# Expert rows added to the residual by accumulating DMA transfers, in a four-layer gated cross-attention kernel

## The chip, the cores and the metric

The kernel runs on one core of a Trainium2 chip. The metric is the time of one execution on the device, in microseconds (us). The engines are PE (matrix multiplication), DVE (vector), ACT (scalar, activation functions), POOL (the general engine, which also issues DMA transfers of its own) and SP (here only an issuer of DMA transfers). Each engine works through its own queue in order and waits at semaphores for the others.

## The reference, cut to what matters

The state `x` is 16 sequences of 128 tokens with 256 features. Four layers follow each other, each a cross attention against a context of 128 positions per sequence (layer 3: 8 heads of 64, layers 0 to 2: 16 heads of 16) and a feed-forward part, both added through a gate:

```python
x = x + jnp.tanh(g_xattn[0]) * _L0_xattn_ref(ctx_1024, _layernorm(x, axis=-1), ctx_1024, ...)
x = x + jnp.tanh(g_ffn[0]) * _L0_ffn_ref(_layernorm(x, axis=-1), ...)
x = x + jnp.tanh(g_xattn[1]) * _L1_xattn_ref(_layernorm(x, axis=-1), ctx_1024, ctx_1024, ...)
...
x = x + jnp.tanh(g_ffn[3]) * _L3_ffn_ref(_layernorm(x, axis=-1), ...)
return x
```

The feed-forward parts of layers 0, 2 and 3 are mixtures of 8 experts; each token goes to its best two, and their outputs are added with the router's weights. In layer 0:

```python
gate = jax.nn.softmax(flat_x @ w_gate.T, axis=-1)
topk_scores, topk_idx = jax.lax.top_k(gate, TOP_K)
cw = (jax.nn.one_hot(topk_idx, N_EXPERTS, dtype=flat_x.dtype) * topk_scores[..., None]).sum(axis=1)
h = jax.nn.gelu(jnp.einsum('td,edh->teh', flat_x, W1) + b1, approximate=False)
y = jnp.einsum('teh,ehd->ted', h, W2) + b2
out = jnp.einsum('ted,te->td', y, cw)
```

Layer 1 has a dense layer with eight low-rank additions instead. In layer 1's attention the softmax runs over the queries and not over the keys.

## The kernel before, in words

The residual lies in SBUF as 16 tiles `xs[b]` of 128 tokens x 256 features, one per sequence. The sequences go in 4 blocks of 4 (NBLK = 4, BPB = 4).

**Attention.** `attend()` (L1282) writes the order of work on PE, ACT, DVE by hand. It walks over the 16 sequences of a layer (of two layers where they follow each other without an expert stage between, layers 1 and 2). A step of a sequence computes scores (ps_s, L1191), exponentials on ACT (e, L1206), sums on DVE (L1215, in layer 1 with v scaled by their reciprocals, L1218 and L1220), the product with v (ps_o, L1246), its copy to SBUF (oT, in layer 1 a DVE copy, L1254), the output projection (ps_y, L1267) and the addition to the residual (L358), after which `ready(b)` takes the mean and variance of the sequence's rows (L237, L238).

Between these, at set points, `tick()` lets *jobs* go on: Python generators which issue a piece of other work and say with `yield n` after how many ticks they want to be called again. The number is capped: `job[1] = min(next(job[0]), most[late])`, with `most` = (5, 1) in layer 0, (99, 1) in layers 1 and 2, (2, 1) in layer 3; `late` is set when the last sequence's step has begun its tail, so that from then on each job goes on at every tick. The jobs are the next block's `prepare` (layer norm, transposes, queries) and the block just finished's `behind` (the router). In the tail, a filler, the first slots of the expert stage, is put in after the jobs of each tick.

**Router.** `front()` (L428) of a mixture takes a block of 4 sequences: layer norm (ACT xn, L298), `yield 4` (L315), transposes on PE (ps_ln, L321), router matmuls (L405), the two largest (DVE, up to `both`, L456), `yield 6` (L457), rank matmuls (ps_rank, L461), then 8 indirect DMAs from POOL (L516) that scatter the block's rows into `xg` in DRAM, sorted by expert. A `plan` (L572 to L660, DVE) says which slot has which expert; plans are made early after the blocks, and the last after block 3.

**Slots.** `slots()` (L671) works on 39 slots of 128 rows of one expert: SP loads the rows (xr, L733) and the expert's weights (1 MB each, L1352), `turn(s)` transposes the rows on PE (ps_xr, L766) and copies them on DVE (xT, L768), `hidden` makes the hidden activations (L1399 in layer 0, L1624 in layer 3), `finish` multiplies with the second weight (ps_e, L803), weighs the rows on DVE (y, L809 and L811) and scatters them from POOL into `yd` in DRAM (L815). There `yd` has two rows per token, one per expert. The first slots (9 in layer 0, 17 in layer 3) run as filler in the attention's tail while later blocks still are being routed; the rest follow. Before slot 0's hidden matmuls stand `turn(0)` and `turn(1)` (L831, L832; `turn` is L760).

**Fetch.** The next layer's attention (layers 1 and 3) first has to add these rows. `fetch()` (L541) does it in `prepare` of each block: SP loads the two rows of each token (yr, 256 KB per sequence, L547), four ticks later two DVE additions per sequence (L552), `ready(b)`, and a tick between sequences. After layer 3, `last()` (L525) does the same on DVE and POOL and stores the output.

**POOL** zeroes `xg` at the start by direct DMAs (L2149), issues the scatters, clears the v tiles of an attention (L1105) and adds up sums or reciprocals of each sequence (`watch.see`, L1060, tile sum_range) for a check of the range; the tiles which it reads have two buffers. If the values leave the range, a second, slower path is run; the fast one (`run["fast"]`) is the one measured.

Of the kernel before, what the change touches and what calls it, by code (L numbers as in the profile page):

```python
# [12 lines left out]
ALU = mybir.AluOpType  # L13
# [7 lines left out]
B = 16  # L21
S = 128
D = 256
KC = D // P
NBLK = 4
BPB = B // NBLK
# [64 lines left out]
def kernel(ctx: ExitStack, tc: tile.TileContext, a: dict, out: bass.AP):  # L91
    nc = tc.nc
# [11 lines left out]
    xs = []  # L104
# [96 lines left out]

    def finish(job):

        while True:
            try:
                next(job)
            except StopIteration as end:
                return end.value  # L210
# [35 lines left out]
    def ready(b):  # L246

        blk, i = divmod(b, BPB)
        if run["fast"]:
            if i == 0:  # L250
                seen[blk] = new_mv()
            mean_var(seen[blk], i, xs[b])
# [52 lines left out]
    def block(blk):  # L305
        return range(blk * BPB, (blk + 1) * BPB)

    def ln_block(blk, see=None, own_set=False):


        mv, rstd = yield from ln_residual(blk, own_set=own_set)
        if see is not None:
            see(rstd)
        xns = yield from normalized([xs[b] for b in block(blk)], mv, rstd)
        yield 4  # L315
        xt = xtpool.tile([P, KC, TB], F32, tag="xnT", name="xnT")
        for pair in range(BPB // 2):
            ps = ps_x.tile([P, KC, 2 * S], F32, tag="x", name="ps_ln")
            for j in range(2):
                for k in range(KC):  # L320
                    nc.tensor.transpose(  # L321
                        ps[:, k, j * S:(j + 1) * S],
                        xns[:, pair * 2 + j, k * P:(k + 1) * P], ident,
                    )
            nc.scalar.copy(xt[:, :, pair * 2 * S:(pair + 1) * 2 * S], ps)
            yield 1 if pair == 0 else 3
        return xns, xt
# [86 lines left out]
    class Moe:  # L414
# [13 lines left out]
        def front(self, blk, plan=None):  # L428
# [25 lines left out]
            first_max(hot[:, 1], key2)  # L454
            both = small("both")
            nc.vector.tensor_tensor(both, hot[:, 0], hot[:, 1], ALU.add)  # L456
            yield 6  # L457


            ps = ps_x.tile([P, 2, BPB, NE], F32, tag="x", name="ps_rank")  # L460
# [79 lines left out]

        def fetch(self, pool, blk):  # L541

            rows2 = yd[:, :].rearrange("(j t) d -> t j d", j=2)
            ys = []
            for b in block(blk):
                y = pool.tile([P, 2, D], F32, tag="yr", name="yr", bufs=BPB)
                nc.sync.dma_start(out=y, in_=rows2[b * S:(b + 1) * S])  # L547
                ys.append(y)
            yield 4
            for i, b in enumerate(block(blk)):  # L550
                for j in range(2):
                    nc.vector.tensor_tensor(xs[b], xs[b], ys[i][:, j], ALU.add)  # L552
                ready(b)
                yield 1
# [116 lines left out]
        def slots(self, n, plans, lanes, get, fetch1, fetch2, hidden, nf, far, depth):  # L671
# [27 lines left out]
            def lane(s):  # L699
                return lanes[plan_of(s)[2]]  # L700
# [59 lines left out]
            def turn(s):  # L760
                if s >= n:
                    return
                xr = xrs[s]
                ps = ps_x.tile([P, KC, S], F32, tag="x", name="ps_xr")
                for k in range(KC):
                    nc.tensor.transpose(ps[:, k, :], xr[:, k * P:(k + 1) * P], ident)  # L766
                xT = get("xT", [P, KC, S])
                nc.vector.tensor_copy(xT, ps)  # L768
                xTs[s] = xT
# [59 lines left out]
                load(s)  # L829
            yield 1  # L830
            turn(0)  # L831
            turn(1)  # L832
            weigh(0)
            hidden_of = []
            for s in range(n):
                while not planned(s + far + 1):
                    yield 1
                first(s + near)
                hT = yield from hidden(get, lane(s), xTs.pop(s), lambda *ps: when(s, *ps))
                turn(s + 2)  # L840
                hidden_of.append((s, hT))
                if len(hidden_of) > depth:
                    finish(*hidden_of.pop(0))
                weigh(s + 1)
                load(s + far)
                second(s + near2)
                yield 1
# [230 lines left out]
    class Fast16:  # L1078
# [155 lines left out]
        def values(self, b, tick):  # L1234
            pool, v = self.pool, self.vs[b % 3]
            es = self.es.pop(b)
            oT = pool.tile([P, KC, S], F32, tag="oT", name="oT")


            po = ps_x.tile([P, 2, KC, S], F32, tag="x", name="ps_o")  # L1240
            for i in range(1 if self.layer == 1 else 2):
                for c in range(KC):
                    for e in range(2):
                        for j in range(4):
                            w = ones2[:, e].rearrange("p e d -> p (e d)")
                            nc.tensor.matmul(  # L1246
                                po[32 * j:32 * (j + 1), i, c, :],
                                lhsT=w if i else v[:, c * HPC + 2 * j + e, :],
                                rhs=es[j][:, 2 * c + e, :], start=(e == 0), stop=(e == 1),
                            )  # L1250
                if i == 0:
                    tick()
            if self.layer == 1:
                nc.vector.tensor_copy(oT, po[:, 0])  # L1254
            else:
                rs = pool.tile([P, KC, S], F32, tag="rs", name="rs")
                nc.vector.reciprocal(rs, po[:, 1])  # L1257
                self.watch.see(rs.rearrange("p c s -> p (c s)"))
                nc.vector.tensor_tensor(oT, po[:, 0], rs, ALU.mult)
            self.os[b] = oT  # L1260
            tick()
# [20 lines left out]
    def attend(parts, most=(99, 1), filler=None, open_end=False):  # L1282

        jobs = []  # L1290
        late = False
        filling = []

        def tick():
            for job in list(jobs) + filling:
                job[1] -= 1
                if job[1] <= 0:
                    try:
                        job[1] = min(next(job[0]), most[late])
                    except StopIteration:  # L1300
                        (jobs if job in jobs else filling).remove(job)

        def ahead(att, before, blk):
            made = att.prepare(blk, before(blk) if before is not None else None)
            made = [[job, 0] for job in made]
            jobs.extend(made)
            return made

        steps = [(att, b) for att, _, _ in parts for b in range(B)]
        blocks = [(att, before, behind, blk) for att, before, behind in parts  # L1310
                  for blk in range(NBLK)]
        with tc.manual_schedule(engines=IN_ORDER):
            ln_exp()
            prepared = ahead(*blocks[0][:2], 0)
            for n in range(len(steps) + 2):
                if n == len(steps) - 1 and open_end:
                    next(filler)
                if n == len(steps):
                    late = True
                    if filler is not None:  # L1320
                        filling.append([filler, 0])
                if n < len(steps):
                    if n % BPB == 0:

                        while any(job in jobs for job in prepared):
                            tick()
                        if n // BPB + 1 < len(blocks):
                            att, before, _, blk = blocks[n // BPB + 1]
                            prepared = ahead(att, before, blk)
                    att, b = steps[n]  # L1330
                    att.scores(b, tick)
                if 1 <= n <= len(steps):
                    att, b = steps[n - 1]
                    att.values(b, tick)
                if n >= 2:
                    att, b = steps[n - 2]
                    att.output(b, tick)
                    if b % BPB == BPB - 1:
                        _, _, behind, blk = blocks[(n - 2) // BPB]
                        jobs.append([behind(blk), 0])  # L1340
            while jobs or (filling and not open_end):
                tick()
# [722 lines left out]
    def layers(fast):  # L2065
# [16 lines left out]
        def routed(moe, turns, begin=None):  # L2082


            plans = []

            def make(blk):
                early = blk < NBLK - 1
                kind = str(len(plans)) if early else ""
                plans.append((yield from moe.plan(turns[blk], early, kind)))  # L2090
                if early and begin is not None:
                    begin(plans[-1])

            def behind(blk):
                yield from moe.front(blk, (lambda: make(blk)) if blk in turns else None)

            return behind, plans

# [313 lines left out]
```

## Time and profile before

| what | value |
|---|---|
| median of 14 runs | 1726.52 us (1721.28 to 1737.39) |
| profiled execution: time, span | 1727.62 us, 1725.8 us |
| busy PE, DVE, ACT, POOL | 1576.9, 901.4, 631.7, 285.0 us |
| PE's mean granted clock | 0.953 of full speed |
| stages of the change: end of layer 0's attention | 125 to 215 us |
| layer 1's attention | 440 to 620 us |
| layer 3's attention, its tail | 1250 to 1560, 1560 to 1640 us |
| DVE additions of L552 | 64, 0.42 us each (median) |
| oT copies of layer 1 (L1254) | 16, 0.42 us each (median) |

The page of the profile gives the busy time of each engine, the span in 40 slices, the queues of the DMA engines and the costliest groups of instructions. In groups and timelines a row reads: start, duration, engine, line, operation, output<-inputs, shape, number of instructions merged, and in brackets the idle time of the engine just before and what ended it. "Issue" and "remote" are idle times for which no semaphore is seen. A view by windows gives the busy time of each engine in a stretch, then PE's granted clock, the busy share of the 16 DMA engines and their GB/s.

### The profile page before, as it was taken

What the parts mean: (1) busy time and instruction counts of PE and PEld (TensorE: products, weight loads), DVE (VectorE), ACT (ScalarE), POOL (GpSimd) and SP (SyncE); (2) the same over time, 40 slices, a digit from 0 to 9 for tenths busy, and PEclk for the clock granted to TensorE, in tenths of its full rate; (3) what the DMA queues carried; (4) which work ended last, traced back from release to release, by engine and by line L of the source; (5) the groups of instructions that cost most, each with busy time, mean ns of one, the idle gap of its engine ahead of it and who ended that gap; (6) DMA issues with size and microseconds to landing.
All of it is one profiled execution on the core that took longest, in us unless ns stands there. A gap on an engine that the chain in (4) does not pass through costs nothing.

```text
span 1725.8 us, 34935 instructions
## 1 busy us (share of the span) xinstructions
PE 1576.9 (91%) x12803; PEld 1213.6 (70%) x12803; DVE 901.4 (52%) x2914; ACT 631.7 (37%) x1501; POOL 285.0 (17%) x364
## 2 busy tenths in 40 slices
PE   7986989999988999889999999999999997988892
PEld 4665889999555666655459999999846564667792
DVE  3665422322277766555445555556725545456554
ACT  4533433345344455534224333334533323222010
POOL 4122321112100000221100111111100002023433
PEclk9988999999998999999999999999989998998996
DMA  9505483542210000110054323410220100023856
GB/s 342 204 26 177 146 277 112 196 140 95 71 44 1 1 3 25 39 38 25 25 181 156 127 71 107 144 32 27 96 64 25 38 1 25 1 94 100 270 186 198
DMA packets 110889, 169.69 MB, mean 98 GB/s; under 512 B 16745, under 2 KB 84142, under 8 KB 110704
## 3 DMA queue, kind: packets, MB, share of 16 engines
q1 hardware_dynamic: 92752, 118.67, 21.6%
q0 software_dynamic: 13392, 43.37, 6.6%
q10 hardware_dynamic: 4560, 5.25, 0.9%
q8 instruction: 108, 1.77, 0.4%
q14 instruction: 77, 0.63, 0.1%
HBM read 268.81 MB, written 48.18 MB: 184 GB/s over the span
## 4 chain that ended last, share of the span: by engine, by line
PE 78%; DVE 11%; ACT 3%; issue 3%; DMA 3%; SPq 1%; POOL 0%; DVEq 0%; ACTq 0%
PE ps_w L1576 15%; PE ps_e L803 12%; PE ps_h L1399 7%; PE ps_w L1511 6%; PE ps_qk L1833 5%; PE ps_o L1246 4%; PE ps_v L1942 3%; PE ps_s L1191 2%; PE ps_g L1624 2%; PE ps_u L1624 2%; PE ps_o L1980 2%; PE ps_y L1267 2%; PE ps_q L912 2%; PE ps_k L912 2%; DVE rs L1257 2%
## 5 line engine op out<-in xcount | busy, mean ns | idle before, releaser
L1576 PEld LDWEIGHTS ps_w<-xT,w 128*128 128x128 f32 x2304 | 264.2, 192 | 2.4
L1576 PE MATMUL ps_w<-xT,w 128*128 128x128 f32 x2304 | 265.0, 275 | 0.0
L815 POOL DMA_INDIRECT yd<-y,to x117 | 119.1, 1018 | 568.5 <-DVE c L778 288.0
L803 PE MATMUL ps_e<-w,hT 128*128 128x256 f32 x848 | 199.4, 382 | 2.3 <-DVE hT L1481 1.9
L803 PEld LDWEIGHTS ps_e<-w,hT 128*128 128x128 f32 x848 | 155.6, 192 | 21.9 <-DVE hT L1481 2.8
L1584 ACT ACTIVATE u<-ps_w,b 128x128 f32<-128x128 f32 x312 | 89.3, 368 | 174.9 <-PE ps_w L1576 161.3
L1587 DVE SCALAR_TENSOR_TENSOR m<-ps_w,b,u 128x128 f32<-128x128 f32 x312 | 87.7, 345 | 110.9 <-PE ps_w L1576 92.8
L1399 PE MATMUL ps_h<-xT,w 128*128 128x128 f32 x1120 | 136.1, 280 | 6.8 <-issue 5.2
L1399 PEld LDWEIGHTS ps_h<-xT,w 128*128 128x128 f32 x1120 | 134.2, 196 | 9.3 <-issue 7.8
L1404 ACT ACTIVATE hT<-ps_h,b 128x128 f32<-128x128 f32 x312 | 88.8, 373 | 125.3 <-issue 90.4
L516 POOL DMA_INDIRECT xg<-xn,xi x96 | 94.2, 981 | 147.4 <-issue 51.3
L1511 PE MATMUL ps_w<-xnT,sw 128*128 128x512 f32 x256 | 111.8, 593 | 0.0
L811 DVE SCALAR_TENSOR_TENSOR y<-ps_e,c,bias 128x256 f32<-128x256 f32 x78 | 37.6, 483 | 125.2 <-PE ps_e L803 121.3
L1060 POOL TENSOR_TENSOR sum_range<-sum_range,rs 128x256 f32<-128x256 f32 x48 | 35.1, 732 | 407.0 <-DVE rs L1257 187.6
L1257 DVE RECIPROCAL rs<-ps_o 128x256 f32<-128x256 f32 x32 | 56.2, 1756 | 68.5 <-PE ps_o L1246 45.0
L1511 PEld LDWEIGHTS ps_w<-xnT,sw 128*128 128x128 f32 x256 | 47.9, 190 | 57.3 <-issue 51.2
L768 DVE COPY xT<-ps_xr 128x256 f32<-128x256 f32 x117 | 48.6, 418 | 63.1 <-PE ps_xr L766 55.6
L1191 PE MATMUL ps_s<-qM,kT 32*128 32x256 f32 x768 | 74.7, 428 | 6.2 <-ACT e L1206 4.4
L298 ACT ACTIVATE xn<-x,nmr,rstd 128x256 f32<-128x256 f32 x128 | 67.7, 598 | 28.5 <-DVE nmr L294 26.2
L1206 ACT ACTIVATE e<-ps_s 128x512 f32<-128x512 f32 x128 | 65.8, 602 | 22.9 <-PE ps_s L1191 17.9
L1191 PEld LDWEIGHTS ps_s<-qM,kT 32*128 32x128 f32 x768 | 41.3, 191 | 37.2 <-issue 20.4
L795 ACT ACTIVATE bias<-b,c 128x256 f32<-128x256 f32 x78 | 40.4, 518 | 70.2 <-DMA b<-in_l_b_dram 26.0
(275 smaller groups left out, 2607.6 us busy)
## 6 DMA issues: line engine op xcount, KB each, us to landing
w<-in_l_w_dram SPq DMA_DIRECT2D x156, 1024.0 KB
w<-in_l_w_dram SPq DMA_DIRECT2D x39, 512.0 KB
kT<-in_l_wgu_dram SPq DMA_DIRECT2D x39, 512.0 KB
xg<-zeros POOLq DMA_DIRECT2D x15, 1170.0 KB
yr<-yd SPq DMA_DIRECT2D x40, 256.0 KB
xr<-xg SPq DMA_DIRECT2D x78, 130.0 KB
b<-in_l_b_dram SPq DMA_DIRECT2D x78, 128.0 KB
kT<-in_l_w_dram SPq DMA_DIRECT2D x39, 256.0 KB
```

Of the source, the lines that this page charges most:

```text
L516: self.unordered(nc.gpsimd.indirect_dma_start(out=xg[:, :], in_=xns[:, i, :], in_offset=None, out_offset=bass.IndirectOffsetOnAxis(ap=xi[: ...
L803: nc.tensor.matmul(po, lhsT=hT[:, f, :], rhs=lane(s)["w2"][:, f, :], start=(f == 0), stop=(f == nf - 1),)
L815: self.unordered(nc.gpsimd.indirect_dma_start(out=yd[:, :], in_=y, in_offset=None, out_offset=bass.IndirectOffsetOnAxis(ap=to[:, 0:1], axi ...
L1191: nc.tensor.matmul(pss[j][:, 2 * c:2 * c + 2, :], lhsT=self.kT[blk][part, c, tok], rhs=self.qM[blk][part, c, :, tok], start=True, stop=True,)
L1257: nc.vector.reciprocal(rs, po[:, 1])
L1399: nc.tensor.matmul(ps[:, i, :], lhsT=w["w1"][:, k, f * P:(f + 1) * P], rhs=xT[:, k, :], start=(k == 0), stop=(k == KC - 1),)
L1404: nc.scalar.activation(hT[:, f, :], ps[:, i, :], AF.Gelu, bias=w["b1"][:, f:f + 1])
L1511: nc.tensor.matmul(ps, lhsT=wt[:, k, f * P:(f + 1) * P], rhs=xnT[:, k, :], start=(k == 0), stop=(k == KC - 1),)
L1576: nc.tensor.matmul(ps[:, f, :], lhsT=wt[:, k, s, f * P:(f + 1) * P], rhs=xT[:, k, :], start=(k == 0), stop=(k == KC - 1),)
L1584: nc.scalar.activation(u[:, f, :], pair[0][:, f, :], AF.Identity, bias=w["b1"][:, i:i + 1])
L1587: nc.vector.scalar_tensor_tensor(m1[:, f, :], pair[1][:, f, :], w["b3"][:, i:i + 1], u[:, f, :], ALU.add, ALU.mult,)
L1833: nc.tensor.matmul(ps, lhsT=w[:, k, c * P:(c + 1) * P], rhs=src[:, k, :], start=(k == 0), stop=(k == KC - 1),)
```

## The change

Four edits:

1. In the fast path, `fetch` of block 0 still loads and adds its own rows as before. It also issues, on POOL's queue, 24 DMAs which add the two rows of each token of sequences 4 to 15 to the residual tiles (128 x 256 floats, 128 KB each). For the other blocks only `ready` is left, a tick apart.
2. In `slots`, `turn(1)` moves from before the first slot's hidden matmuls to after them.
3. Layer 1's oT copy goes from DVE to ACT.
4. Distances between stages of `front`: a yield of the class `Firm` is not capped. For the last block (`own_set`) the two distances become 3 and 2 ticks also when `late`; before they were capped to 1 there. In fronts with an early plan every yield is capped to 3 (`quick`).

```diff
+    class Firm(int):
+        pass
+
+    def quick(job):
+
+        for n in job:
+            yield min(n, 3)
...
-        yield 4
+        yield Firm(3) if own_set else 4
...
-            yield 6
+            yield Firm(2) if own_set else 6
...
         def fetch(self, pool, blk):
 
+
+            if run["fast"] and blk > 0:
+                for b in block(blk):
+                    yield 1
+                    ready(b)
+                return
             rows2 = yd[:, :].rearrange("(j t) d -> t j d", j=2)
...
+            if run["fast"]:
+                for b in range(BPB, B):
+                    for j in range(2):
+                        nc.gpsimd.dma_start(
+                            out=xs[b], in_=rows2[b * S:(b + 1) * S, j], accum_op=ALU.add
+                        )
             yield 4
...
             turn(0)
-            turn(1)
             weigh(0)
...
                 hT = yield from hidden(get, lane(s), xTs.pop(s), lambda *ps: when(s, *ps))
+                if s == 0:
+                    turn(1)
                 turn(s + 2)
...
             if self.layer == 1:
-                nc.vector.tensor_copy(oT, po[:, 0])
+                nc.scalar.copy(oT, po[:, 0])
...
-                        job[1] = min(next(job[0]), most[late])
+                        n = next(job[0])
+                        job[1] = n if isinstance(n, Firm) else min(n, most[late])
...
             def behind(blk):
-                yield from moe.front(blk, (lambda: make(blk)) if blk in turns else None)
+                if blk in turns:
+                    job = moe.front(blk, lambda: make(blk))
+                    yield from quick(job) if blk < NBLK - 1 else job
+                else:
+                    yield from moe.front(blk)
```

The instructions in their new order: on POOL the 24 DMAs stand behind the clearing of the v tiles and ahead of the layer's sum_range additions. They go as the first adds of sequences 4 to 8, the second adds of these five (each waits until the first add to the same tile has landed), then 9 to 13 in the same way, then 14 and 15. The first reader of such a tile, L237 on DVE, waits for its second DMA. In layer 1 the oT copy stands on ACT's queue between two pairs of xn or between groups of e. Layer 0's and layer 3's last ps_rank stand about one slot later in PE's order.

## Prediction

> **What bounds the kernel now.** I read the page's busy shares first, then the table by stage, then PE's waits in the stages that the change touches, then the timeline around the longest of these waits.
>
> ```profile
> PE 1576.9 (91%) x12803; PEld 1213.6 (70%) x12803; DVE 901.4 (52%) x2914; ACT 631.7 (37%) x1501; POOL 285.0 (17%) x364
> ...
> PEclk9988999999998999999999999999989998998996
> ```
>
> PE is busy for 91% of 1725.8 us, so only 149 us of the span have no matmul in them. No engine beside PE is over 52%: DVE matters only where PE waits for it, and the granted clock dips (8 and 9 instead of 9 and 9) where such waits lie. The table by stage (columns: window, length, then busy PE, PEld, DVE, ACT, POOL, then clock and DMA share) shows where:
>
> ```profile
> 125.00:215.00 90.00, 72.70 (x662) 63.59 (x655) 44.59 (x196) 38.34 (x91) 23.96 (x27) 0.89 0.46 152
> 470.00:620.00 150.00, 135.56 (x1135) 84.98 (x1137) 116.11 (x315) 68.87 (x141) 6.67 (x16) 0.92 0.05 15
> 1300.00:1560.00 260.00, 242.21 (x2532) 157.79 (x2531) 133.73 (x363) 71.71 (x150) 27.87 (x35) 0.96 0.11 34
> 1560.00:1640.00 80.00, 66.25 (x429) 58.79 (x428) 50.33 (x260) 15.67 (x31) 32.58 (x34) 0.89 0.58 190
> ```
>
> These are the tail of layer 0's attention, layer 1's attention, layer 3's attention and its tail: PE idles 17.3, 14.4, 17.8 and 13.8 us. In 470 to 620 DVE is busy for 77% and ACT for 46%. PE's waits there (440 to 625):
>
> ```profile
> PE ps_ln L321 <- ACT xn L298: 4.4, 3, 2.5
> PE ps_y L1267 <- DVE oT L1254: 4.3, 2, 2.1
> PE ps_ln L321 <- ACT zT L1453: 3.5, 1, 3.5
> PE ps_s L1191 <- ACT e L1206: 2.3, 1, 2.3
> PE ps_o L1246 <- DVE v L1220: 1.0, 2, 0.8
> ```
>
> The timeline of DVE shows why oT is late, the timeline of PE the one long wait of layer 0's tail:
>
> ```profile
> 509.76 0.93 DVE L552 TENSOR_TENSOR x<-x,yr 128x256 f32<-128x256 f32 x2
> ...
> 511.29 0.85 DVE L552 TENSOR_TENSOR x<-x,yr 128x256 f32<-128x256 f32 x2
> ...
> 512.74 0.39 DVE L1254 COPY oT<-ps_o 128x256 f32<-128x256 f32 x1
> ```
>
> ```profile
> 160.48 0.66 PE L766 MATMUL ps_xr<-ident,xr 128*128 128x128 f32 x2 [7.16 <-DMA xr<-xg]
> 160.94 3.62 PE L1399 MATMUL ps_h<-xT,w 128*128 128x128 f32 x16
> ```
>
> The adds of the next block's expert rows stand ahead of this block's oT. And PE, in order, waits 7.16 us for the second slot's rows although the matmuls behind (first slot) don't need them.
>
> **The change, part by part.** All terms are against the profiled execution (1727.62 us, span 1725.8). It lies 1.1 above the median of the 14 runs, 1726.52; the same difference is taken from the median at the end.
>
> *turn(1) after slot 0's hidden matmuls.* The 7.16 us wait no longer holds them. What is late next is their weight: 1 MB issued at 148.33. In the DMA view about 1 MB has moved by 153.3 (282 to 419 GB/s from 150 to 152.5), so slot 0 can start near 154 instead of 160.94: 6.5 us, and the end of the low clock (0.56 in 160 to 165, after a window of no matmul). xr1 landed at 160.3, when slot 0 and the two interleaved ps_o and ps_y groups (5 to 7 us) end: no new wait to speak of. Ends: 0 (the weight itself lands at 160.9) and 9 us. I take 6.5.
>
> *Firm and quick.* Block 3's transposes and rank matmuls come 3 and 2 ticks after the yield instead of 1. In the order of the instructions layer 0's last rank goes from before slot 5's hidden matmuls (208.2) to before slot 6's, about 7.2 us later in order. The rank releases eight scatters (213 to 223), then the last plan (228.46); SP issues the next rows of a slot at 235.40, so 7 us lie between. When all before it comes 6.5 us earlier and the plan 0.7 later, some of this slack is spent: I give back 3 us (ends 0 and 6.5). In layer 3's tail the 2.4 us wait of ps_rank for DVE's both (1591.91) is covered by a slot, but the last plan comes two slots of 2.87 us later: ends -2.4 and +5.7, taken as 0. The first wait there, 4.31 us for xn at 1573.65, stays, since ps_ln stands at the same place in the order. Layer 2 is ordered as before but for a few instructions: 0.
>
> *Layer 1: 24 adds leave DVE, 16 oT copies go to ACT.* 24 x 0.42 = 10.1 us and 16 x 0.41 = 6.6 us off DVE's 116; ACT gains 16 copies of about 0.59 (its row of xnT copies has twice the elements), at most 9.4 on 69. The waits that can end at this DVE work are ps_y for oT (2.13 at 513.18 and 549.66), ps_s for e (2.27 at 483.42, just after two pairs of adds), ps_o for v (1.0) and one of ps_ln for xn (0.64 at 515.93; the 2.5 is block 0's, the third lies behind the last add of 548.2): 8.2 us. Not all goes: oT stands among xn and e on ACT's queue, and the chain from e over sums to v stays. The 1.78 us of adds ahead of oT at 509.76 to 512.14 are less than its wait, but oT's queue on DVE goes too. I take 5; ends 0 and 8.2. DVE's bn_stats (L237) now waits for the tile's second DMA, and queued behind it are the running block's sums, v and residual; if the DMA is early, the wait is nothing.
>
> *Layer 3: 24 adds.* Another 10.1 us. The waits on their path are ps_kv for xn, 2.40 (1359.21) and 3.92 (1437.96), and ps_v for oT, 2.77 (1427.40). Two pairs of adds (0.85 us each) lie late in each of these chains: I take 4 (ends 0 and 9.1).
>
> *24 DMAs per layer on POOL.* POOL is free: its v memsets end at 446.7, its next work is sum_range at 478.43. A direct DMA from POOL takes 0.72 us at best in this trace (the zeroing of xg), an indirect one 1.28 with its gap: 24 take 17 to 31 us, 446.7 to 464 or 478. 3072 rows of 1 KB at 64 ns (hardware queue: 21.6% of 16 engines over 92752 packets) are 12 us on 16 engines. The five tiles of the first group have both adds after 10 DMAs, by 459.5 plus a landing of some 3 us (last scatter to yr: 3.35 us), and block 1's first add was at 471.07. In layer 3: 1253 plus 13 plus 3, against 1298.11. So both are hidden by 8 and 29 us. sum_range now waits behind 24 DMAs, at worst until 478, its own time. The price of the sharing with block 0's yr loads is unknown: 0 to 6 us (the 12 us of packets, interleaved half and half, against the 5.8 us by which ACT's lv, at 458.01, came after DVE's ve of 452.19); the nearest row, DMA share 0.05 to 0.09 in this stretch, speaks for little: 1. The 24 SP loads of yr and their slots go, off the path: 0.
>
> Sum: -6.5 + 3 - 5 - 4 + 1 = **-11.5 us**: 1716.1 for the profiled execution, 1715 for the median.
>
> A rule against it: the Trainium skill, "SBUF — State Buffer", section "Who interferes with whom" and its box on SWDGE, says that a DMA issued from GpSimd is held up while VectorE copies in a two-port mode, 0.62 us alone and 3.1 beside it. The scatters of 135 to 140 kept 0.97 us with DVE busy 4.62 of 5 us, which speaks against it as far as it goes: little of that DVE work was a copy. By that rule the time would be rival 3's.
>
> **Rivals.**
>
> *1. The waits only change hands (same).* DVE loses work, but PE waits as long for ACT: oT is put between two pairs of xn on ACT's queue, and xn waits for DVE's rstd chain (ACT sat idle 2.61 us before xn at 487.44). For it: ACT e is already a releaser. Against it: ACT is at 46%. Then only the layer 0 tail remains, -3.5 + 1: 1724 for the median.
>
> *2. Bursts on POOL stall the other engines (slower).* Ends of bursts of eight scatters coincide with stalls that no semaphore explains (the last scatter of a burst on POOL's timeline, then DVE's timeline beside it):
>
> ```profile
> 1446.63 0.97 POOL L516 DMA_INDIRECT xg<-xn,xi  x1 [0.30 <-issue]
> ```
>
> ```profile
> 1449.19 0.69 DVE L1999 TENSOR_TENSOR oT<-ps_o,rs 128x512 f32<-128x512 f32 x1 [9.26 <-remote]
> ```
>
> and at 147.65 DVE had been idle 5.27 us at the end of the burst of 135 to 145. The change adds 48 DMAs in two bursts, six times eight. At 5 us per eight they cost 30: 1715 + 30 = 1745. From 11.5 / 6 = 1.9 us per eight it makes the kernel slower. For it: four of some twelve bursts are followed by 5 to 9 us. Against it: the other bursts cost under 3 us, the 15 direct DMAs of the zeroing none on PE, and in 440 to 460 layer 1 has 5.8 us of slack.
>
> *3. Each DMA of the burst takes some 3 us (slower).* Then 24 take 74 us, 446.7 to 521; block 1's ten are there at 478 instead of 471, and sum_range waits until 521, with two buffers for what it reads (tile sums): the third sequence's DVE work waits from 494, 27 us. 1715 + 27 = 1742. The rows of 0.72 to 1.0 us speak against it.
>
> *4. More is gained.* Where waits go the clock recovers: 460 to 500 and 520 to 560 ran at 0.83 to 0.84, 1425 to 1465 at 0.82 to 0.84. A dip costs up to 16% of 20 us of matmuls, 3 us per window; three of six windows give 9: 1706.
>
> **How the numbers follow.** Forecast 0.54, rival 1 0.20, rival 2 0.13, rival 3 0.04, rival 4 0.09. About 0.3% (5 us) is what a measurement of this kernel can tell from no change. The forecast's own spread, by its ends (layer 1 0 to 8.2, layer 3 0 to 9.1, tail 0 to 9 less what is given back), of which I take about half on each side, reaches from 1708 to 1721. Faster by over 0.3% (below 1721): forecast and rival 4, 0.63. Within: rival 1, 0.20. Slower: rivals 2 and 3, 0.17. The range 1702 to 1734 leaves out the larger part of the slower rivals (0.13) and the best of rival 4 (0.04).
>
> **What would show it.** Right: PE's 7.16 us wait for xr gone and hidden matmuls near 154; no L552 adds after 452 in layer 1, oT on ACT, ps_y's 4.3 us gone, PE's idle time in 470 to 620 some 9 us instead of 14.4; POOL's 24 DMAs done by 478, bn_stats without a wait for DMA. Wrong: "issue" or "remote" idle times of 5 us beside these DMAs; yr of block 0 landing later than ACT's lv (458.01); ps_y waiting for ACT's oT; layer 0's later slots waiting for the last plan by over 3 us.

## Result, and the profile after

The changed kernel takes 1702.47 us (median; 1692.95 to 1704.78) against 1728.27 of the kernel before: a ratio of 0.983, 95% interval 0.9808 to 0.9853 (the plain quotient of the two medians is 0.985, at the upper end of the interval). By the medians that is 25.8 us less. The forecast had 11.5 us less (1715): the right side, but less than half of what came. Beside other runs it was measured twice more, with ratios of 0.9815 (0.9793 to 0.9838) and 0.983 (0.9809 to 0.985). Its profiled execution took 1696.81 us, span 1695.0.

The page after, in the lines that answer to those of before:

```profile
PE 1559.3 (92%) x12803; PEld 1205.6 (71%) x12803; DVE 875.8 (52%) x2850; ACT 636.4 (38%) x1517; POOL 327.4 (19%) x412
...
PEclk8988999999999999989999999999989999999896
```

PE runs the same 12803 matmuls in 17.6 us less busy time. Less busy time for the same matmuls points at the clock that PE was granted. To place the gain, each PE instruction of one trace was matched with the same one of the other. The table has, for three pairs, by how much the median difference in start time changes over each stage (before against after; the same kernels again, on one chip, r_before and r_after; and e13, whose time is that of before, against the changed kernel's third profile, r_after_2):

```
gain by stage, us         layer 0   layer 1   layer 2   layer 3   last slots
first pair                  -9.0     -11.2      +6.3     -15.8      -1.4
second pair                 -9.1     -11.1      -2.9     -16.8      +3.1
e13 against r_after_2      -10.4      -9.2      -3.1      -9.3      +1.3
forecast                    -3.5      -4         0        -4         0
```

Layer 2 differs between pairs in both directions; nothing is built on it. Layer 0 has a spread of its own: e10, whose layer 0 is the changed kernel's, gains 12.5 us there against e13. The other three stages each brought more than twice what was forecast.

Layer 1, from its first ps_k to its last ps_l, by windows of before and then of after (columns as in the table by stage):

```profile
440.10:684.10 244.00, 224.73 (x1881) 138.29 (x1879) 162.61 (x440) 117.47 (x227) 14.91 (x29) 0.94 0.08 23
```

```profile
430.30:663.20 232.90, 214.24 (x1881) 133.10 (x1880) 147.19 (x400) 121.51 (x243) 35.88 (x53) 0.98 0.13 24
```

The stage is 11.1 us shorter and PE's busy time 10.5: the idle time hardly changed. The clock rose from 0.94 to 0.98. The waits of PE after (430 to 605) say the same:

```profile
PE ps_ln L329 <- ACT xn L306: 5.7, 4, 2.5
PE ps_zT L1471 <- ACT oT L1275: 1.9, 1, 1.9
PE ps_ln L329 <- ACT oT L1275: 1.9, 1, 1.9
PE ps_y L1288 <- ACT oT L1275: 1.7, 2, 0.9
PE ps_o L1267 <- DVE v L1241: 1.5, 2, 0.8
```

The waits did change hands, from DVE's oT to ACT's, as rival 1 said; but they are spread out more: the longest of the list is 2.5 us, where it was 3.5.

The clock in the trace is granted in stretches that are whole multiples of 3.41 us, at full or at half, nothing between. In before, two windows with long waits and what follows each:

```profile
546.70:550.10 3.40, 1.27 (x34) 0.98 (x26) 3.12 (x12) 0.00 (x0) 0.00 (x0) 1.00 0.00 0
550.10:553.50 3.40, 3.40 (x11) 2.07 (x10) 2.67 (x13) 0.87 (x3) 0.00 (x0) 0.51 0.02 5
553.60:557.00 3.40, 0.42 (x4) 0.15 (x2) 2.29 (x4) 3.40 (x9) 0.00 (x0) 1.00 0.00 0
557.00:560.40 3.40, 2.84 (x15) 1.86 (x16) 2.58 (x9) 1.50 (x5) 0.42 (x1) 0.50 0.00 0
```

PE was busy 1.27 and 0.42 us of 3.4, and the next window ran at half clock: 11 matmuls fill 3.4 us. After, at the same work, PE is busy for over half of each window, and no half clock follows:

```profile
531.10:534.50 3.40, 1.87 (x29) 1.14 (x21) 3.05 (x15) 0.67 (x3) 0.00 (x0) 1.00 0.00 0
534.50:537.90 3.40, 1.74 (x8) 1.05 (x8) 1.01 (x4) 3.06 (x7) 0.00 (x0) 1.00 0.02 5
537.90:541.30 3.40, 2.15 (x24) 1.50 (x24) 3.30 (x8) 2.79 (x6) 0.42 (x1) 1.00 0.00 0
```

So a stage's length can be split into matmuls at full clock, idle time of PE, and half of the time in which PE is busy at half clock. From the first pair of traces:

```
                      length   idle   half-clock time   PE busy in it   rest
layer 0, before        380.1   31.4        37.5             27.1       335.2
layer 0, after         370.3   24.2        30.7             25.5       333.3
layer 1, before        244.3   19.3        30.7             28.9       210.6
layer 1, after         233.2   18.7        10.2              9.3       209.9
layer 3, before        241.1   14.5        26.5             24.8       214.1
layer 3, after         220.6    6.4         8.8              8.2       210.1
```

(Layer 0 from 60 us to layer 1's first ps_k; layer 3 from its first to its last ps_qk, without the tail; rest is length less idle time less half of the busy time at half clock.) Layer 1's 11.1 us are 0.6 of idle time and 9.8 of clock. Layer 3's 20.5 are 8.1 of idle time and 8.3 of clock, and 4.0 that this split does not explain; what follows it then takes 5 us longer than before, so that less is left in the table above. Layer 0 is another case: of its 9.8 us, 7.2 are idle time and 0.8 clock, and in the third pair idle time fell by 10.7 us and the clock brought 0.2; in the second pair the clock has a share (4.6 of idle time, 5.4 of clock). Of layer 3's 9.1 us of waits for xn and oT 2.4 are left; first before (1300 to 1560), then after (1284 to 1430):

```profile
PE ps_kv L1809 <- ACT xn L298: 6.3, 2, 3.9
PE ps_v L1942 <- DVE oT L1999: 2.8, 1, 2.8
```

```profile
PE ps_v L1964 <- DVE oT L2021: 1.5, 1, 1.5
PE ps_kv L1831 <- ACT xn L306: 0.9, 2, 0.7
```

POOL's timeline shows the DMAs of layer 1 (merged rows: x5 is five DMAs):

```profile
436.90 4.47 POOL L566 DMA_DIRECT2D x<-yd  x5
443.12 14.92 POOL L566 DMA_DIRECT2D x<-yd  x17 [1.75 <-DMA x<-yd]
460.31 1.72 POOL L566 DMA_DIRECT2D x<-yd  x2 [2.27 <-DMA x<-yd]
467.33 0.24 POOL L1081 TENSOR_TENSOR sum_range<-sum_range,sums 128x32 f32<-128x32 f32 x1 [5.30 <-DVE sums L1239]
```

This is 0.88 us each (a row's time by its number; the records of single DMAs overlap and last 0.84 to 3.3 us). All are issued by 462, 5.3 us before POOL's next work. No bn_stats (L245) waited for one of them, and PE has no idle time without a semaphore in the whole of layer 1.

### The profile page after: what moved, and what is told of

The parts are those of the page before. It is cut to its first block, busy times and chain, and to the rows that moved or that the text cites. A ratio compares the mean times of both kernels' runs of the same rounds, so it can differ in the third digit from the quotient of the medians.

```text
span 1695.0 us, 34913 instructions
## 1 busy us (share of the span) xinstructions
PE 1559.3 (92%) x12803; PEld 1205.6 (71%) x12803; DVE 875.8 (52%) x2850; ACT 636.4 (38%) x1517; POOL 327.4 (19%) x412
## 4 chain that ended last, share of the span: by engine, by line
PE 76%; DVE 12%; ACT 4%; DMA 3%; issue 2%; another core or an unknown queue 1%; SPq 1%; POOL 1%; DVEq 0%; ACTq 0%
PE ps_w L1598 15%; PE ps_e L823 12%; PE ps_h L1421 7%; PE ps_w L1533 6%; PE ps_qk L1855 5%; PE ps_o L1267 3%; PE ps_v L1964 3%; PE ps_s L1212 2%; DVE rs L1278 2%; PE ps_g L1646 2%; PE ps_k L933 2%; PE ps_u L1646 2%; PE ps_router L413 2%; PE ps_s L1985 2%; PE ps_y L2031 2%
## 5 line engine op out<-in xcount | busy, mean ns | idle before, releaser
L1533 PE MATMUL ps_w<-xnT,sw 128*128 128x512 f32 x256 | 115.8, 610 | 0.0
L1212 PEld LDWEIGHTS ps_s<-qM,kT 32*128 32x128 f32 x768 | 42.2, 193 | 34.3 <-issue 20.4
```

What stands on the lines that cost most here:

```text
L1212: nc.tensor.matmul(pss[j][:, 2 * c:2 * c + 2, :], lhsT=self.kT[blk][part, c, tok], rhs=self.qM[blk][part, c, :, tok], start=True, stop=True,)
L1533: nc.tensor.matmul(ps, lhsT=wt[:, k, f * P:(f + 1) * P], rhs=xnT[:, k, :], start=(k == 0), stop=(k == KC - 1),)
```

## The experiments

The theory after the result: the parts cure long waits of PE, and a long wait can cost twice, its idle time and the half clock behind it. The main rival: only the idle time counts. Ratios are to the kernel before on the same chip at the same time. That matters: before took 1728 and 1741 us in two of the groups of runs and 1686 to 1688 in all others (see the last section).

**e1: the accumulating DMAs alone** (before with the edit of `fetch`)

```diff
+            if run["fast"] and blk > 0:
+                for b in block(blk):
+                    yield 1
+                    ready(b)
+                return
...
+                        nc.gpsimd.dma_start(
+                            out=xs[b], in_=rows2[b * S:(b + 1) * S, j], accum_op=ALU.add
+                        )
```

> The kernel before with the accumulating DMAs alone (oT stays on DVE, turn(1) and the distances as before). Theory A (clock): the larger part of the gain in layers 1 and 3 is that short idle windows of PE no longer bring half clock; half-clock time falls from 30.7 us to some 15 in layer 1's attention (460 to 565) and from 17 us to under 4 in layer 3's (1350 to 1455), and the time falls by 12 to 18 us, over half of it as shorter matmuls. Theory B (waits alone): PE's busy time stays and the time falls by 5 to 9 us. Theory C (it is the oT copy that matters in layer 1): layer 1 keeps its time, 6 to 10 us in layer 3 alone.

Measured: 1672.0 against 1686.22, ratio 0.9923 (0.9904 to 0.9943): 13 us less (the ratio's 0.77% of 1686). By stage against e13: layer 1 -6.4, layer 3 -10.3 us. Half-clock time in layer 1 is 13.7 us and idle time 20.4, more than before's 19.3. Theory A holds for layer 1; in layer 3, idle time is 6.4 us instead of 12.3, so both count. Theory C falls. (In e7, the same kernel again, half-clock time in layer 1 is 20.5 us, idle time 19.1, and the gain there 5.1.)

**e2: turn(1) alone**

```diff
             turn(0)
-            turn(1)
...
+                if s == 0:
+                    turn(1)
                 turn(s + 2)
```

> The kernel before with turn(1) moved alone. The wait of 7.2 us for xr goes, the hidden matmuls of slot 0 start about 7 us earlier and find the clock up a window earlier. Theory A: 7 to 9 us less, since the last ranks stay early and nothing is given back. Theory B (the weights of the next slots or the last plan are late next): 2 to 4 us less, with a new wait for w or the plan before 245.

Measured: 0.9971 (0.9957 to 0.9985), 4.3 us less, just above theory B's 2 to 4, whose new wait for w is there. The trace has 7.4 us less at the end of layer 0 (against e13) and gives 0.9 back in layer 1 and 1.0 in the last slots. Waits of 6.9 us for w and 3.4 for xr stand where a kernel without the part (e3) has 13.5 for xr and 2.3 for w.

**e3: the oT copy alone**

```diff
-                nc.vector.tensor_copy(oT, po[:, 0])
+                nc.scalar.copy(oT, po[:, 0])
```

> The kernel before with layer 1's oT copy on ACT alone. Theory A: the two waits of 2.1 us for oT shrink, and one or both of the half-clock stretches behind them (519 and 550 to 564) go: 3 to 7 us less, all of it before 620. Theory B (waits alone): 2 to 4 us less. Theory C (ACT's queue holds oT up as long as DVE's did): within 1 us of before.

Measured: 1.0014 (0.9998 to 1.003). By the ratio it is 2.4 us slower, with an interval that reaches 0: alone the move gains nothing, which is nearest to theory C. PE now waits 3.0 us in one place for ACT's oT.

**e4: Firm and quick alone; e12: quick alone; e13: Firm alone**

```diff
+    def quick(job):
+
+        for n in job:
+            yield min(n, 3)
...
+                    yield from quick(job) if blk < NBLK - 1 else job
```

(e12; e13 has the lines with `Firm` instead, e4 both.)

> The kernel before with the stage distances alone (Firm and quick). Theory A: the 6 us which the changed kernel lost between 715 and 820 (layer 2's last block) come from the later ranks there, so this kernel is 2 to 8 us slower there, and gains 0 to 3 in layer 3's tail. Theory B: that loss came from the phase of the clock's windows, and this kernel is within 3 us of before there, and as a whole.

> The kernel before with the cap of 3 ticks in fronts with an early plan alone (quick). Theory A: it brings the whole 9 us which Firm and quick gained together, all before layer 1, since block 1's plan is ready earlier and slot 0's rows are issued some 10 us earlier. Theory B (Firm brings it): within 2 us of before.

> The kernel before with block 3's distances of 3 and 2 ticks alone (Firm, without quick). Theory A: within 2 us of before until layer 1, 0 to 3 us less in layer 3's tail. Theory B: it brings the 9 us of layer 0's tail. The prediction had it cost 3 us in layer 0's tail and nothing in layer 3's.

Measured: together 0.9955 (0.9938 to 0.9972), quick 0.9957 (0.9943 to 0.9972), Firm 0.9996 (0.9983 to 1.0009). Quick brings all of it. Neither theory of e4 held: there was no loss in layer 2, and the whole was 8 us faster. e12 is nearest to its theory A, with 7 us instead of 9 and slot 0's rows issued 5 us earlier instead of 10; e13 is within 2 us of before, so its theory B falls. SP's timeline shows what quick does; first without it (e13), then with it alone (e12), the load of slot 0's rows:

```profile
139.58 0.37 SPq L736 DMA_DIRECT2D xr<-xg  x1
```

```profile
134.30 0.36 SPq L738 DMA_DIRECT2D xr<-xg  x1
```

Block 1's front in layer 0 asks for up to 5 ticks between its steps. With 3, its rank matmuls come at 115.12 instead of 117.98, its plan is ready 5 us earlier (127.92 instead of 132.87), and so the first slots' rows and weights are issued 5 us earlier. PE's waits for xr in layer 0's tail (120 to 215) are 13.7 us in e13 and 7.0 in e12: the same stretch that turn(1) cures from the other side. Of the 7 us of e12, 4.4 are seen in layer 0 of its trace.

**e5: the changed kernel without Firm and quick; the changed kernel beside it**

> The changed kernel without Firm and quick. Theory A (overlap in layer 0's tail): it is 2 to 5 us slower than the changed kernel, since turn(1) alone takes most of that wait away. Theory B (no overlap): 8 to 10 us slower, as much as Firm and quick gained alone. Theory C (Firm costs in layer 2's last block, as the first pair of profiles showed 6 us there): faster than the changed kernel.

> The changed kernel once more, on one chip with the runs beside it. Theory A (the parts add up but for an overlap: turn(1) and quick cure the same wait in layer 0's tail, 4 and 9 us of which 4 count once): 1.2 to 1.4% less than before. Theory B (the parts add up in full): 1.6% or more.

Measured: e5 0.984 (0.9815 to 0.9865), slower than the changed kernel (0.9815, 0.9793 to 0.9838) by 6 us of the medians, 4.4 by the ratios, with intervals that overlap. That is theory A of e5 or a little above it. For r_after it is theory B: 1.85% less, so the large overlap that theory A expected is not there. How far turn(1) and quick overlap stays open. By the traces the first takes 7.4 us off layer 0, the second 4.4, both 9 to 10 in the changed kernel and 12.5 to 13.7 in e10 and e14; beside e5, on its chip, quick and Firm add only 1 us there.

**e6, and e7 with e8 on one chip: what the 48 DMAs cost.** e7 is e1 once more. e6 and e8 leave the addition out:

```diff
+            if run["fast"] and blk > 0:
+                for b in block(blk):
+                    yield 1
+                    ready(b)
+                return
```

> The kernel before, with the expert rows of blocks 1 to 3 neither loaded nor added in layers 1 and 3 (this part of the computation is left out), and no DMA in their place. Against the run with the accumulating DMAs alone (0.77% less than before) it gives the price of the 48 DMAs. Theory A (they are hidden): 0.7 to 0.9% less than before. Theory B (each burst costs PE some us): 1.1% less or more.

> The accumulating DMAs alone, now on one chip with the run that leaves the additions out. Theory A (the DMAs are hidden): the ratio to before is that of the run beside it within 0.2%. Theory B (each burst of 24 costs PE 3 us or more): 0.35% or more above it, with idle time of PE at 445 to 470 or 1255 to 1300 that the run beside it lacks.

> The kernel before, with the expert rows of blocks 1 to 3 neither loaded nor added in layers 1 and 3 (this part of the computation is left out) and no DMA in their place, beside the accumulating DMAs alone. Theory A: the same ratio as beside it within 0.2%. Theory B: 0.35% or more below it.

Measured: e6 0.9886 (0.9866 to 0.9906) beside e5 and the changed kernel; e7 0.9917 (0.9896 to 0.9938) and e8 0.9905 (0.9884 to 0.9927) on one chip. The last two differ by 0.12%, 2 us and inside both intervals, and layer 1 takes 237.4 us in both traces: within the measurement the DMAs are hidden, as theory A of e7 and e8 has it. e6 taken alone would have said theory B (1.14% less against e1's 0.77% on another chip). e6's lower ratio was measured while before took 1741 us, and the changed kernel, too, had its lowest ratio there.

**r_before: before once more, beside these**

> The kernel before once more, for a profile on the chip of the runs beside it. The profiles of the four parts showed almost no stall behind the bursts of scatters, where the first profile of before had several of 2 to 8 us. Theory A (it is the chip): this profile has them or lacks them like the three others of this call. Theory B: it is the kernel, and this profile has them where the changed kernels don't.

Measured: 1745.43 us, with the stalls; the three kernels beside it have them too, and so did the two traces of the first pair; no kernel of the other groups has any. So it is not the kernel, as theory A has it; but the same chip later ran e7 to e10 without them, so it is not the chip as such either.

**e9 and e11: useless matmuls ahead of the waits.** All additions stay on DVE; PE gets more to do. e11's places in layer 3, for example:

```diff
                 ps = ps_x.tile([P, KC, 2 * S], F32, tag="x", name="ps_kv")
+                for _ in range(warm if run["fast"] and pair == 0 else 0):
+                    nc.tensor.matmul(
+                        ps[:, 0, :], lhsT=ident, rhs=self.w[3][:, 0, :], start=True, stop=True
+                    )
```

> The kernel before with 30 useless matmuls (about 14 us of PE at full clock, overwritten by the real ones) ahead of six of PE's waits: ps_y of sequences 3 and 7 and ps_v of sequence 2 in layer 1, ps_kv of blocks 2 and 3 and ps_v of sequence 9 in layer 3. Every addition stays on DVE and every wait ends when it did. Theory A (clock): the half-clock stretches behind these waits go (17 us of half clock in layer 1, 17 in layer 3), and the time falls by 6 to 15 us. Theory B (waits alone): the time stays or grows by up to 4 us, the useless matmuls that overrun the waits.

> The kernel before with 28 useless matmuls (about 13 us of PE at full clock, overwritten or unused), now ahead of the waits themselves: in layer 1 three before ps_o of sequences 3 and 7 (in the unused half of its tile) and four before ps_v of sequence 2, in layer 3 five before ps_kv of block 1, eight before ps_kv of block 2, five before ps_v of sequence 9. Nothing else is changed. From the start of layer 1's attention to its last ps_l a quiet run takes 243 us, from layer 3's first ps_qk to its last 233. Theory A (half clock is a cost of its own): the half-clock stretches there go from some 30 to 10 us and from 20 to 10, and each stage loses 3 to 8 us although PE has more to do. Theory B (the next wait takes over, since DVE and ACT hold the pace): the half clock goes and the stages keep their time within 2 us. Theory C (the matmuls delay their own successors): both grow by 4 us or more.

Measured: e9 1.0037 (1.0022 to 1.0052), e11 1.006 (1.0042 to 1.0078): both slower, by 6 and 10 us; theory A's times were missed, and e9 lies above its theory B too. In e11 layer 1 keeps its time (theory B), layer 3 grows by 6 us (theory C). e9's matmuls stood at blocks that do not wait in layer 3, and in layer 1 those for ps_y waited themselves. Its layer 1 still tells something. By windows, e13 (for before) and e9:

```profile
428.10:670.30 242.20, 223.09 (x1881) 138.19 (x1879) 162.23 (x440) 117.57 (x227) 14.91 (x29) 0.94 0.08 23
```

```profile
428.10:668.40 240.30, 219.63 (x1906) 137.32 (x1905) 162.10 (x440) 117.22 (x227) 14.94 (x29) 0.99 0.08 23
```

With the same work on DVE and ACT, more matmuls (x1906; a few records are missing) and 1.6 us more idle time, the stage is 1.9 us shorter and PE's busy time 3.5 us less, because half-clock time fell from 27.3 to 6.8 us. So half clock is a cost of its own. Layer 3 says the same without useless matmuls: in the eleven traces whose additions are off DVE (with DMAs in their place, or none), its idle time is 6.4 to 6.5 us in each, its half-clock time differs, and its length goes with it: 217.4 us at none (e8, e14), 219.9 and 220.1 at 6.8 us (e1, e10), 220.6 to 221.9 at 8.8 to 10.2 us (the other seven). It was not worth buying with matmuls: the useless matmuls cost most of it in layer 1, and in layer 3 (both kernels) 6 us more than they brought. Idle time there fell only from 12.3 to 9.9 us; the chain from PE over DVE and ACT to the next xn probably moved back with PE.

**e10, e14, e15 and the changed kernel once more: which parts are needed.** e10 is the changed kernel with oT on DVE, e14 without Firm, e15 without both.

> The changed kernel with layer 1's oT copy back on DVE. Alone the move changed nothing. Theory A (with the additions gone DVE has room, so ACT against DVE is nothing): within 2 us of the changed kernel. Theory B (the two add up in layer 1: 6.5 us without the move, 10.5 with it, by the profiles of one chip): 3 to 5 us slower than the changed kernel, all of it between 470 and 620.

> The changed kernel with quick but with block 3's distances as before (without Firm). Theory A (Firm gives back in layer 0's tail): 1 to 4 us faster than the changed kernel, 1.75 to 2.0% less than before. Theory B (Firm helps in the tails): 1.4 to 1.6% less than before.

> The changed kernel beside the smallest version. Theory A (Firm and the oT copy are worth 1 to 3 us each where all else is in place): 1.75 to 2.0% less than before. Theory B (they are worth nothing): 1.6 to 1.75%, like the two leave-out runs.

> The kernel before with the accumulating DMAs, turn(1) after the first slot and quick; without Firm and with oT on DVE. Theory A: 3 to 6 us slower than the changed kernel. Theory B: within 2 us of it. The parts alone gave 0.8 (DMAs), 0.3 (turn) and 0.4% (quick), 1.5% in all.

Measured: e10 0.9834 (0.9813 to 0.9854), e14 0.9833 (0.9813 to 0.9853), the changed kernel 0.983 (0.9809 to 0.985), e15 0.9853 (0.9831 to 0.9875). e10 is as theory A has it, e14 lies between its two, the changed kernel within theory B, e15 within theory A. One of the two may go at no measurable price; without both the medians are 4.2 us apart on one chip (1662.01 and 1657.78), with intervals that still overlap. In layer 1 the idle time of PE is the same with oT on DVE (19.1 us, e10) and on ACT (18.3, r_after_2); half-clock time is 20.5 and 13.7. The traces show what the medians can't: with the DMAs in place, layer 1 takes 236.1 to 237.6 us in the four with oT on DVE (e1, e7, e10, e15) and 233.0 to 234.4 in the five with oT on ACT (the changed kernel's three, e5, e14). So the copy is worth some 3 us there once the additions are gone, and nothing before (e3). No version beats the changed kernel by more than the measurement can tell.

## Why the prediction was wrong, point by point

- **What bounds the kernel**: right. The gain came out of PE's waits in the three stages named.
- **turn(1)**: mechanism and size right. Alone (e2) the forecast's 6.5 is 7.4 us in layer 0, and slot 0 then waits 4.0 us for its weight, as forecast. In the changed kernel its matmuls start at 151.02, where the whole shift until there is 2.8 us, and the weight has landed, issued at 142.72 instead of 148.33:

```profile
151.02 2.73 PE L1421 MATMUL ps_h<-xT,w 128*128 128x128 f32 x16 [0.52 <-DVE xT L788]
```

- **Firm and quick**: the step "I give back 3 us" was not borne out, and quick was put at nothing without a reason, which is the larger miss. Firm alone is nothing (0.9996; by the interval between 3 us faster and 1.5 slower), and the changed kernel without it (e14) has the same ratio. Quick brings 7 us (0.43%) by itself, through the plan of block 1, not through block 3. Instead of -6.5 + 3 layer 0 gave -9 to -10.
- **Layer 1, "I take 5"**: this step failed: the term was argued from the wrong view. The list of waits was read as if a wait cost its length. The idle time stayed (19.3 and 18.7 us), and what went was the half clock behind the longest waits, 30.7 to 10.2 us, worth 9.8. The prediction had this as rival 4 at 0.09, "3 us per window; three of six windows give 9", and left it out of the sum. The DMAs alone bring 5.1 to 6.4 us of the 11 (e1, e7), the oT copy the rest, together with them only.
- **Layer 3, "I take 4"**: mis-sized. 24 additions take 10.1 us off DVE, and 6.7 of the 9.1 us of waits went with them, plus 8.3 us of clock that had no term. The layer gains 9.3 us in the third pair, without stalls, and 16 in the first two, where before also had 7 to 8 us more of the stalls of the last section.
- **The 48 DMAs, "1"**: right that they are hidden (e7 against e8: 2 us apart, inside the intervals). They took 0.88 us each, inside the estimate of 0.72 to 1.28, so rival 3 did not come about. This is no test of the rule of the Trainium skill's "SBUF — State Buffer" ("A bandwidth-pool intuition that's wrong (but worth ruling out)"), 3.1 us beside a copy on DVE: DVE ran additions beside the first DMAs (436 to 442), and until 460 no copy.
- **Rival 2**: no stall beside the new bursts. The stalls are real and lie near the scatters, but not in every run; and its reading that no semaphore explains them was wrong: DVE waits for PE there (last section).
- **Rival 1** happened in part: PE waits 5.5 us in all for ACT's oT, no less than the 4.7 for DVE's before. But little half clock followed them: 6.8 us at the work of 470 to 620, against 23.9 before.

The forecast's own condition "PE's idle time in 470 to 620 some 9 us" was not met (13.7 us by the windows; 13.8 at the same work, 459 to 599), though that stretch became 9.8 us shorter. For layer 1 the idle time was the wrong measure.

## What to carry to other kernels

Price a wait of PE with what follows it: look at the granted clock in the window behind it, and add half of PE's busy time at half clock to the idle time. A change that splits one long wait into several short ones can gain as much as one that removes it; layer 1 is the case. It need not be so everywhere: layer 0's gain was mostly idle time. And where a change touches the distances of several stages, follow each one to the DMA that it releases; the one without a term in the sum may be the one that pays.

## What the runs showed of the hardware

**The clock.** In the twenty traces, of the 3.41 us windows of the clock's record at full clock in which PE was busy for less than 40%, all 186 were followed by half clock; from 40 to 50%, 61 of 90; from 50 to 60%, 51 of 175; from 60 to 70%, 5 of 123; above that, 67 of 8452. Half clock needs no empty window. The Trainium skill, "TensorE: Matmul & The Clock Gate", "Part 1: The HAM clock gate", has the two states and a free-running window of 3413 ns, which agrees with the clock's stretches here; it speaks of an idle window, which these counts widen. That the windows run free may be why one kernel (e1, e7) has 13.7 us of half clock in layer 1 in one run and 20.5 in another, with 20.4 and 19.1 us of idle time; this was not tested.

**Stalls that come and go.** In the first two pairs DVE and ACT stood still for up to 9.4 us (DVE) near the end of a burst of scatters. In before's second trace, POOL's last scatter and DVE beside it:

```profile
1459.67 0.97 POOL L516 DMA_INDIRECT xg<-xn,xi  x1 [0.31 <-issue]
```

```profile
1462.40 0.69 DVE L1999 TENSOR_TENSOR oT<-ps_o,rs 128x512 f32<-128x512 f32 x1 [9.42 <-remote]
```

The view says remote because it can't put the semaphore down to an instruction; there is a semaphore, and it is the one that PE's matmuls count up. In e13 the same instruction waits for PE as well, and for 2.20 us only:

```profile
1417.42 0.69 DVE L2003 TENSOR_TENSOR oT<-ps_o,rs 128x512 f32<-128x512 f32 x1 [2.20 <-PE ps_o L1984]
```

What falters is PE. In e13 its 64 ps_o matmuls run in one go of 2.98 us; in before's second trace 58 do, and the other six come a few at a time, with idle time between for which no semaphore is seen:

```profile
1452.12 3.29 PE L1980 MATMUL ps_o<-e,v 128*32 128x128 f32 x58
1456.42 0.38 PE L1980 MATMUL ps_o<-e,v 128*32 128x128 f32 x3 [1.00 <-issue]
1457.15 0.27 PE L1980 MATMUL ps_o<-e,v 128*32 128x128 f32 x1 [0.35 <-issue]
```

Such idle time of PE sums to 28.4 and 30.2 us in the two traces of before, to 14.8 and 19.8 in the two of the changed kernel, to 28.6 and 29.3 in e5 and e6, and to 0.6 to 1.9 in the other fourteen traces. Layer 1 has none in any trace. In layer 3 with its tail and the last slots it is 10.5 and 12.0 us in before against 3.5 and 4.3 in the changed kernel. This difference of 7 to 8 us is about what layer 3 gained more in the first two pairs (16 us) than in the third (9), and the 28 us are about half of the difference between before's profiled 1745 and e13's 1687 us. What makes PE falter in some runs and not in others is open.
